# One gather tile in 64 fetched row by row on SyncE's queue, layer 0's last steps reordered, a drain behind the last gather

## The chip, the cores and the metric

The kernel runs on one core of a Trainium2 chip. The metric is device time in microseconds, the median of several executions. A core has five engines that run side by side, each with an instruction queue in order: PE (TensorE, matrix products), DVE (VectorE), ACT (ScalarE), POOL (GpSimd) and SP (SyncE, which only issues transfers). Transfers run on the core's DMA engines and report by semaphores.

## The reference: what is computed

The kernel computes two layers of a relational graph convolution over a graph of 12,500 nodes with 128 features each, 200,000 edges sorted by destination, and 8 edge types (relations), and then a layer norm:

```python
def conv(h, src, dst, et, basis, comp, root, bias):
    W = einsum('rb,bio->rio', comp, basis)            # 8 matrices 128x128
    msgs = einsum('ni,rio->nro', h, W)[src, et]       # one row of 128 per edge
    mean = per (dst, et): sum of msgs / max(count, 1)
    return mean.sum over the 8 relations + h @ root + bias

h = x
for l in range(2):
    h = relu(conv(h, ...layer l...)) + h
out = layernorm(x + h)                                # over the 128 features, eps 1e-5
```

All data is float32. x, src, dst and the edge types are inputs; the weights are basis, comp, root and bias of each layer.

## The kernel before

**Tiles.** The edges are taken in order, 128 to a tile: T = 1563 tiles, the last with 64 edges. Four tiles make a quad (Q = 4, NQ = 391 quads, the last with three tiles), eight make a group (G = 8). The 12,500 nodes make NT = 98 blocks of 128; on average a block's edges fill 16 tiles, that is four quads. Because the edges are sorted by destination, a tile's edges go to few nodes, and the kernel counts on that (a slower `general_path` stands behind a flag that is read at the very end and is not taken here).

**How the work is ordered.** Nearly every operation is recorded in a plan, with what it reads and writes; the plan is then emitted, each engine's operations in the order in which they were recorded, with semaphore waits put in where one operation needs another's result or its buffer. So the order of the Python calls is the order of each engine's queue. Transfers go out on SP's queue through the helper `load` (line 565), which all of them share.

**The gathers.** `gather(l, q)` fetches the rows of one quad, one indirect DMA per tile (line 583): POOL makes the 128 descriptors from 128 indices in SBUF, which lie one per partition. Layer 0 reads rows of x by the edge's source node; layer 1 reads rows of y_d, a DRAM array of 8 x 12,500 rows that layer 0 has written, by source x 8 + type. Behind each gather stands a memset into a scratch tile, `pace` (line 589), 256 columns wide in layer 0 and 200 in layer 1, and each memset waits for the one eight back. The rows of a quad land in one of 14 buffers; gathers are recorded 12 quads ahead of their readers (AHEAD = 12).

**Layer 0** (loop from line 1117). For quad q: `onehot` (DVE, line 873) builds a 128 x 128 matrix per tile from precomputed positions and weights 1/count; `means` (PE, line 914) multiplies the rows by it, ACT copies the result to SBUF; per group `product` (PE, line 938, 16 passes for 8 relations) applies the relation matrices and `place` (PE, line 961) adds the group's result into the block's accumulator. `close_block` (lines 974 to 989) finishes a node block: DVE adds the bias, applies relu and adds the old rows; then three steps are put on the list `todo`, and one is taken from it in each of three quads out of four: `turn` (PE transpose, ACT copy to y_col, store to hT_d), `half(0)` and `half(1)` (PE, line 986: the block times four of layer 1's relation matrices each, into the same PSUM bank pt; ACT copies each to y_row; after the second, one store of the block's 1024 rows to y_d).

**Between the layers.** The loop covers all 391 quads. Behind it stand the place and close of block 96, the last product, the rest of `todo`, and the place and close of block 97. Layer 1's first gather waits for all stores to y_d.

**Layer 1** (loop from line 1163). `onehot` builds 128 x 256 matrices; `add_rows` (PE, line 1028) multiplies a tile's rows by them straight into the accumulator of one block and its neighbour, and adds the block times the root matrix (line 1031) once. `finish(k)` (ACT line 1040, DVE 1047 and 1048) adds what the previous block left over, relu and the old rows; `norm(k)` (PE transpose line 1062, DVE 1063 to 1069, ACT 1066) adds x, applies the layer norm and stores to out. `norm(k)` is recorded behind the first quad of the next block. `load2(k + 1)` fetches the next block's hT_d and x on SP's queue.

**The end.** After the plan the engines meet; a drain of POOL that the framework puts there stands first (line 1185), then each engine reads the flag into a register (line 1212) and branches.

Of the kernel before, what the change touches and what calls it, by code (L numbers as in the profile page):

```python
# [8 lines left out]
F32 = mybir.dt.float32  # L9
# [3 lines left out]
ALU = mybir.AluOpType  # L13
# [286 lines left out]
class Plan:  # L300
# [83 lines left out]
    last = None  # L384
# [31 lines left out]
def ordered_path(  # L416
# [21 lines left out]

    nc = tc.nc
    P = 128
    N, D = x.shape
# [16 lines left out]
    C = P + 2 * HALO  # L460
    S4 = 4
    AHEAD = 12
    H = R // 2
    assert D == P and R * K == P and B == BF + 1 and 1 < TL and LAST < P and BF % 4 == 0
    main = slice(HALO, HALO + P)

    const = ctx.enter_context(tc.tile_pool(name="const", bufs=1))
# [36 lines left out]
    sel = keep([P, G, K], F32, "sel")  # L504
    spread = keep([P, B, GB], F32, "spread")

    PACE, PACED = 8, (2 * P, 200)
    pace = keep([P, PACE, 2 * P], F32, "pace")
    paced = tc.alloc_semaphore("s_paced")
    key = keep([P, 4, C], F16, "key")  # L510
    low = keep([P, 4, C], I32, "low")
    eqs = Ring(const, 2, [P, S4, 4, C], F16, "eq")
    turns = Ring(const, 3, [P, 4, P], F32, "tu")
    rows_r = Ring(const, AHEAD + 2, [P, Q, D], F32, "rows")
    dm_r = Ring(const, 4, [P, Q, 2 * P], F32, "dm")
    sT_r = Ring(const, 3, [P, R, G, K], F32, "sT")
    pl_r = Ring(const, 3, [P, 2 * P], F32, "pl")
# [49 lines left out]
    def copy(out_t, in_t, reads, writes):  # L567
        act(lambda: nc.scalar.activation(out_t, in_t, AF.Copy), reads, writes)  # L568

    rows_g = {}  # L570

    def gather(l, q):
        if q >= NQ:
            return
        t, cell = rows_r.take()
        rows_g[l, q] = (t, cell)
        ids = idx if l == 0 else idy

        def emit():
            ins = []  # L580
            for i in range(q * Q, min((q + 1) * Q, T)):
                m = LAST if i == T - 1 else P
                ins.append(nc.gpsimd.indirect_dma_start(  # L583
                    out=t[:m, i - q * Q, :], out_offset=None, in_=x if l == 0 else y_d,
                    in_offset=bass.IndirectOffsetOnAxis(ap=ids[:m, i:i + 1], axis=0)))
                k = l * T + i
                if k >= PACE:
                    nc.gpsimd.wait_ge(paced, k - PACE + 1)
                nc.gpsimd.memset(pace[:, k % PACE, :PACED[l]], 0).then_inc(paced, 1)  # L589
            return ins  # L590

        b = q * Q // P
        reads = ["idx0" if l == 0 and q == 0 else ("idx", b)] if l == 0 else [("idy", b)]
        if l == 1 and q == 0:
            reads += [("y_d", j) for j in range(NT)]
        plan.add("POOL", emit, reads, [cell], lane="gq", n=min(Q, T - q * Q))

    def weight(l, r):
        c0 = (l * R + r) * NB
# [306 lines left out]
    def means(q):  # L906
        t, c = rows_g.pop((0, q))
        d, dc = dms.pop((0, q))
        s, sc = s_b[q % 2]

        def emit():
            for i in range(in_quad(q)):
                m = LAST if q * Q + i == T - 1 else P
                last = nc.tensor.matmul(s[:, i, :], t[:m, i, :], d[:m, i, :P], start=True, stop=True)  # L914
# [54 lines left out]
    def close_block(j):  # L969
        n = rows_of(j)  # L970
        p, pc = po[j]
        t, c = h_in.pop(j)
        h, hc = h_r.take()
        vec(lambda: nc.vector.tensor_add(h[:n], p[:n], bias_sb[:n]), [pc, "bias"], [hc])  # L974
        vec(lambda: nc.vector.scalar_tensor_tensor(h[:n], h[:n], 0.0, t[:n], op0=ALU.max, op1=ALU.add), [c], [hc])
        pt, pc2 = pt_b
        yc, ycc = yc_r.take()
        yr, yrc = yr_r.take()

        def turn():  # L980
            pe(lambda: nc.tensor.transpose(pt[:, 0, :n], h[:n, :], ident[:n, :n]), [hc, "ident"], [pc2])
            copy(yc[:, :n], pt[:, 0, :n], [pc2], [ycc])
            load(hT_d[j * P:(j + 1) * P, :n], yc[:, :n], [ycc], [("hT_d", j)])

        def half(k):
            pe(lambda: nc.tensor.matmul(pt[:n].rearrange("p r d -> p (r d)"), yc[:, :n],  # L986
                                        w_sb[:, 1, k * H:(k + 1) * H, :].rearrange("p r d -> p (r d)"),
                                        start=True, stop=True),
               [ycc] + [("w", 1, r) for r in range(k * H, (k + 1) * H)], [pc2])
            copy(yr[:n, k * H:(k + 1) * H, :], pt[:n], [pc2], [yrc + (k,)])  # L990
            if k == 1:
                load(y_d[j * P * R:(j * P + n) * R, :].rearrange("(p r) d -> p (r d)", r=R),
                     yr[:n].rearrange("p r d -> p (r d)"), [yrc + (0,), yrc + (1,)], [("y_d", j)])

        todo.extend([turn, lambda: half(0), lambda: half(1)])
# [7 lines left out]
             (ct_b[0].rearrange("p t d -> p (t d)")[:, :2 * P], ct_b[1])]  # L1003

    def load2(k):
        if not 0 <= k < NT:
            return
        n = rows_of(k)
        t, c = hTs[k] = hin_r.take()
        load(t[:, :n], hT_d[k * P:(k + 1) * P, :n], [("hT_d", k)], [c])  # L1010
        t, c = xs[k] = xs_r.take()
        load(t[:n], x[k * P:k * P + n, :], [], [c])

    def add_rows(q, k, opens, last):
# [2 lines left out]
        a, ac = acc[k]  # L1017
        n = in_quad(q)
        root_in = opens and k >= 0
        reads = [c, dc]  # L1020
        if root_in:
            ht, hc = hTs[k]
            reads += [hc, ("w", 1, R)]
# [1 line left out]
        def emit():  # L1025
            for i in range(n):
                m = LAST if q * Q + i == T - 1 else P
                ins = nc.tensor.matmul(a, t[:m, i, :], d[:m, i, :], start=(opens and i == 0),  # L1028
                                       stop=(last and i == n - 1))
# [84 lines left out]
    later = [lambda b=b: check_edges(b) for b in range(B)]  # L1114
    later += [check_span, check_place, check_all]
    later.reverse()
    for q in range(NQ):
        g = q * Q // G
        gather(0, q + AHEAD)
        onehot(0, q + 2)  # L1120
        if q == 1:
            where()
# [22 lines left out]
                parts = None  # L1145
        elif later:
            later.pop()()
    g = NG - 1
# [93 lines left out]
```

## Time and profile before

| | us |
|---|---|
| median of 15 runs | 4561.1 (4553.16 to 4581.48) |
| the profiled execution | 4560.43 |
| its span, first to last instruction | 4558.6 |
| POOL's gathers of layer 0, first to last | 3.45 to 2278.95 |
| POOL's gathers of layer 1, first to last | 2299.56 to 4516.86 |
| last store to out issued | 4540.81 |

| engine | busy us | share of the span |
|---|---|---|
| PE | 2535.3 | 56% |
| DVE | 1708.0 | 37% |
| ACT | 521.3 | 11% |
| POOL | 3939.3 | 86% |

In the profile's lines L583 is line 583 of the kernel; a tile's name stands without its buffer number. "POOL rows L583 <- issue" means that POOL was idle ahead of a gather without waiting for anything that the profile shows; "remote" is a releaser that it could not name. A "q" behind an engine's name (SPq, POOLq) is that engine's sequencer, which issues transfers and runs register and semaphore instructions. All queues together moved 295.88 MB, of which the gathers' software queue had 205.00 MB and kept the 16 DMA engines busy for 15.9% of the span, the other loads and stores 86.62 MB and 5.7%.

### The profile page before, as it was taken

To read this page: it belongs to the slowest core of one execution; us is meant where nothing else is said; L and a number is where in the kernel's file an instruction comes from. 1 tells how busy PE (TensorE), PEld (TensorE's weight loads), DVE (VectorE), ACT (ScalarE), POOL (GpSimd) and SP (SyncE) were. 2 spreads that over 40 slices of the span, in tenths; PEclk is the share of its full clock that TensorE was granted. 3 is DMA by queue.
4 is the path that set the end of the run, shared out by engine and by line. 5 is a ranking of instruction groups with operands and counts; after the bars stand their busy time and mean duration, and the time that the engine had idled before them with its cause. 6 is when DMAs were issued, how large, how long until landed. Compare 5 with 4: busy or idle time off the path is not lost.

```text
span 4558.6 us, 38109 instructions
## 1 busy us (share of the span) xinstructions
PE 2535.3 (56%) x11691; PEld 2045.3 (45%) x11691; DVE 1708.0 (37%) x4724; ACT 521.3 (11%) x1190; POOL 3939.3 (86%) x6260
## 2 busy tenths in 40 slices
PE   4776666666766666666653435435435444435444
PEld 3565555555655555555532324324333333324333
DVE  8772222222222222222232434435334443434434
ACT  0122212222121221211100000000000000000000
POOL 8888888888888888888878888888888888888885
PEclk7998778777788888888776777667667777767767
DMA  3222222222222222222221112111111211112111
GB/s 89 61 84 75 75 74 75 75 75 75 75 80 74 71 75 75 75 75 75 74 60 53 57 53 57 55 53 57 55 54 55 57 55 55 55 54 57 55 53 41
DMA packets 193416, 295.88 MB, mean 65 GB/s; under 512 B 60725, under 2 KB 130687, under 8 KB 193203
## 3 DMA queue, kind: packets, MB, share of 16 engines
q0 software_dynamic: 100032, 205.00, 15.9%
q1 hardware_dynamic: 90650, 86.62, 5.7%
q8 instruction: 96, 1.57, 0.1%
q10 hardware_dynamic: 2521, 1.73, 0.1%
q14 instruction: 117, 0.96, 0.1%
HBM read 229.11 MB, written 64.00 MB: 64 GB/s over the span
## 4 chain that ended last, share of the span: by engine, by line
POOL 40%; another core or an unknown queue 21%; issue 16%; DVE 15%; PE 7%; ACT 1%; DMA 0%; POOLq 0%; ACTq 0%; DVEq 0%; SPq 0%
POOL rows L583 30%; POOL pace L589 10%; DVE dm L873 10%; PE s L1028 2%; PE ct L1028 1%; DVE w_sb L607 1%; PE ct L715 1%; PE ct L716 1%; DVE eq L709 1%; PE s L914 1%; DVE y_col L1047 1%; PE y L938 1%; DVE h L1063 1%; DVE ys L1069 1%
## 5 line engine op out<-in xcount | busy, mean ns | idle before, releaser
L583 POOL DMA_INDIRECT rows<-y_d,idy x1563 | 1489.8, 953 | 309.5 <-issue 254.9
L583 POOL DMA_INDIRECT rows<-in_x_dram,idx x1563 | 1499.6, 959 | 265.0 <-issue 254.3
L589 POOL MEMSET pace<- 128x256 f32 (+1 forms) x3126 | 954.6, 305 | 2.3
L1028 PE MATMUL s<-dm,rows 128*128 128x256 f32 x2086 | 677.3, 487 | 298.5 <-DVE dm L873 171.2
L873 DVE TENSOR_SCALAR dm<-cols,near,w 128x256 f32<-128x256 f32 x1563 | 728.2, 534 | 244.2 <-remote 214.4
L873 DVE TENSOR_SCALAR dm<-cols,kr,w 128x128 f32<-128x128 f32 x1563 | 527.8, 401 | 469.5 <-remote 178.5
L1028 PEld LDWEIGHTS s<-dm,rows 128*128 128x128 f32 x2086 | 510.7, 255 | 423.8 <-DVE dm L873 189.1
L914 PE MATMUL s<-dm,rows 128*128 128x128 f32 x3126 | 536.2, 327 | 290.0 <-DMA rows<-in_x_dram,idx 273.6
L914 PEld LDWEIGHTS s<-dm,rows 128*128 128x128 f32 x3126 | 496.6, 236 | 439.4 <-DMA rows<-in_x_dram,idx 284.6
L938 PE MATMUL y<-w_sb,sT 128*128 128x128 f32 x3136 | 517.5, 335 | 4.4 <-issue 4.2
L938 PEld LDWEIGHTS y<-w_sb,sT 128*128 128x128 f32 x3136 | 507.4, 253 | 6.8 <-issue 6.6
L1062 PE MATMUL po<-ident,y_col 128*128 128x128 f32 x98 | 40.4, 412 | 736.3 <-DVE y_col L1047 368.0
L1028 PE MATMUL ct<-dm,rows 128*128 128x256 f32 x1040 | 329.9, 473 | 181.1 <-DVE dm L873 146.2
L974 DVE TENSOR_TENSOR h<-po,bias_sb 128x128 f32<-128x128 f32 x98 | 28.5, 291 | 949.7 <-PE s L914 431.5
L1062 PEld LDWEIGHTS po<-ident,y_col 128*128 128x128 f32 x98 | 16.2, 165 | 772.4 <-DVE y_col L1047 385.4
L1028 PEld LDWEIGHTS ct<-dm,rows 128*128 128x128 f32 x1040 | 244.9, 247 | 243.2 <-DVE dm L873 157.8
L568 ACT ACTIVATE sT<-s 128x512 f32<-128x512 f32 x391 | 233.4, 597 | 871.6 <-PE s L914 378.3
L961 PE MATMUL po<-ys,pl 128*128 128x128 f32 x780 | 156.6, 331 | 312.7 <-ACT ys L568 271.8
L961 PEld LDWEIGHTS po<-ys,pl 128*128 128x128 f32 x780 | 120.3, 221 | 339.6 <-ACT ys L568 292.5
L986 PE MATMUL pt<-w_sb,y_col 128*128 128x512 f32 x392 | 234.2, 683 | 7.0 <-ACT y_col L568 2.0
L1063 DVE TENSOR_TENSOR h<-po,xs 128x128 f32<-128x128 f32 x98 | 28.2, 288 | 422.3 <-remote 331.3
L1047 DVE TENSOR_TENSOR y_col<-s,hT 128x128 f32<-128x128 f32 x66 | 18.9, 287 | 392.0 <-issue 221.7
(121 smaller groups left out, 1301.1 us busy)
## 6 DMA issues: line engine op xcount, KB each, us to landing
y_d<-y_row SPq DMA_DIRECT2D x97, 512.0 KB
rows<-in_x_dram,idx POOLq DMA_INDIRECT x1563
rows<-y_d,idy POOLq DMA_INDIRECT x1563
h_in<-in_x_dram SPq DMA_DIRECT2D x98, 64.0 KB
h_in<-hT_d SPq DMA_DIRECT2D x98, 64.0 KB
xs<-in_x_dram SPq DMA_DIRECT2D x98, 64.0 KB
hT_d<-y_col SPq DMA_DIRECT2D x97, 64.0 KB
out_dram<-ys SPq DMA_DIRECT2D x97, 64.0 KB
```

Of the source, the lines that this page charges most:

```text
L568: act(lambda: nc.scalar.activation(out_t, in_t, AF.Copy), reads, writes)
L583: ins.append(nc.gpsimd.indirect_dma_start(out=t[:m, i - q * Q, :], out_offset=None, in_=x if l == 0 else y_d, in_offset=bass.IndirectOffse ...
L589: nc.gpsimd.memset(pace[:, k % PACE, :PACED[l]], 0).then_inc(paced, 1)
L873: last = nc.vector.tensor_scalar(t[:, i - q * Q, :wide], cols[:, :wide], ids[:, i:i + 1], w[:, i:i + 1], op0=ALU.is_equal, op1=ALU.mult)
L914: last = nc.tensor.matmul(s[:, i, :], t[:m, i, :], d[:m, i, :P], start=True, stop=True)
L938: last = nc.tensor.matmul(y[:m], t[:, r, :nt, :].rearrange("p t k -> p (t k)"), w_sb[:, 0, r, :], start=(r == 0), stop=(r == R - 1))
L961: last = nc.tensor.matmul(po[j][0][:n], t[:m, k * P:k * P + n], o[:m], start=False, stop=(j in closed))
L986: pe(lambda: nc.tensor.matmul(pt[:n].rearrange("p r d -> p (r d)"), yc[:, :n], w_sb[:, 1, k * H:(k + 1) * H, :].rearrange("p r d -> p (r d)"),
L1028: ins = nc.tensor.matmul(a, t[:m, i, :], d[:m, i, :], start=(opens and i == 0), stop=(last and i == n - 1))
L1047: vec(lambda: nc.vector.tensor_add(v[:, :n], a[:, :n], t[:, :n]), [ac, c], [vc])
L1062: pe(lambda: nc.tensor.transpose(p[:n, :], v[:, :n], ident), [vc, "ident"], [pc])
L1063: vec(lambda: nc.vector.tensor_add(h[:n], p[:n, :], xt[:n]), [pc, xc], [hc])
```

## The change

**One tile in 64 goes another way.** With FAR = 16 quads, the last tile of every sixteenth quad (tile numbers 63, 127, ... up to 1535: 24 of them in each layer) is left out of `gather`, with its memset. Its 128 rows are fetched one by one on SP's queue instead, by `fetch`: at each quad of the loop SP loads BITE = 8 indices from src_i in SBUF into 8 registers, and for each of them computes a row's address and issues a transfer of one row of 512 bytes from x or y_d to one partition of a tile of its own (two such buffers, farSP). Sixteen fetches make a tile; the fetch at quad q belongs to a tile that is read LEAD = 8 quads later, or up to fifteen quads after that for its first pieces. The first eight fetches of each layer are recorded ahead of its loop. `means` and `add_rows` read such a tile from its own buffer and wait for its sixteen pieces.

SP's queue has 14,126 instructions instead of 1,072; POOL's has 48 gathers and 48 memsets fewer. Fetches stand in SP's queue between the stores and loads of their quad, in order with them.

**Indices for layer 1.** One new DVE instruction behind layer 0's loop turns src_i into source x 8 + type in place (128 x 1536).

**Layer 0's last steps.** The loop stops before the last quad. Then: the rest of `todo`, block 96's last product, place and close, `todo` down to one step, the last quad's `means`, that last step, the last product, the place and close of block 97. For the last block the second half goes to the PSUM bank ct instead of pt, DVE copies it instead of ACT, and each half has a store of its own.

**Layer 1.** `load2(1)` is recorded up front with `load2(0)`; in the last quad `norm(96)` stands ahead of `add_rows`.

**The drain.** POOL gets a drain instruction right behind the last gather's quad.

```diff
+    FAR, LEAD = 16, 8
+    BITE = P // FAR
-    PACE, PACED = 8, (2 * P, 200)
+    PACE, PACED = 8, (256, 200)
+    n_paced = [0]
+    far_r = {e: Ring(const, 2, [P, D], F32, f"far{e}") for e in ("SP", "ACT")}
-    plan = Plan(tc, {"hw": 8, "aq": 4, "gq": 3})
+    plan = Plan(tc, {"hw": 8, "aq": 4, "gq": 3, "rSP": 4, "rACT": 4})
+    far_at = {"SP": FAR - 1}
+    row_regs = {e: [plan.engines[e].alloc_register(f"row{k}") for k in range(BITE)] for e in far_at}
+    def far(i):
+        for e, at in far_at.items():
+            if i % (FAR * Q) == at * Q + Q - 1 and i < BF * P and (at == FAR - 1 or i >= FAR * Q):
+                return e
+        return None
+
+    def fetch(e, l, q, part=0, parts=1):
+        s = q + LEAD + FAR - 1 - far_at[e]
+        i, c = (s // FAR * FAR + far_at[e]) * Q + Q - 1, s % FAR
+        if far(i) != e:
+            return
+        if c == 0 and part == 0:
+            far_g[l, i] = far_r[e].take()
+        t, cell = far_g[l, i]
+        n = BITE // parts
+        eng = plan.engines[e]
+        regs = row_regs[e]
+
+        def emit():
+            if part == 0:
+                eng.load(regs, src_i[i % P:i % P + 1, i // P, c * BITE:(c + 1) * BITE])
+            ins = []
+            for k in range(part * n, part * n + n):
+                at = eng.snap(regs[k], min_val=0, max_val=(N if l == 0 else N * R) - 1)
+                p = c * BITE + k
+                ins.append(eng.dma_start(t[p:p + 1, :], (x if l == 0 else y_d)[bass.ds(at, 1), :]))
+            return ins
+
+        reads = [("src", i // P)]
+        if l == 1 and i < 2 * FAR * Q:
+            reads += [("y_d", j) for j in range(NT)] + [("y_d", NT - 1, 1)]
+        plan.add(e, emit, reads, [cell + (c, part)], lane="r" + e, n=n)
+
+    def bits(l, i):
+        return [far_g[l, i][1] + (c, part) for c in range(FAR) for part in range(2)] if far(i) else []
+        tiles = [i for i in range(q * Q, min((q + 1) * Q, T)) if not far(i)]
-            for i in range(q * Q, min((q + 1) * Q, T)):
+            for i in tiles:
-                k = l * T + i
+                k = n_paced[0]
+                n_paced[0] += 1
...
+                rows = far_g[0, q * Q + i][0] if far(q * Q + i) else t[:, i, :]
-        pe(emit, [c, dc], [sc])
+        pe(emit, [c, dc] + bits(0, q * Q + Q - 1), [sc])
...
+            hb, hc2 = ct_b if j == NT - 1 and k == 1 else pt_b
+            if j == NT - 1:
+                if k == 0:
+                    copy(yr[:n, :H, :], hb[:n], [hc2], [yrc + (k,)])
+                else:
+                    vec(lambda: nc.vector.tensor_copy(yr[:n, H:, :], hb[:n]), [hc2], [yrc + (k,)])
+                load(y_d[j * P * R:(j * P + n) * R, :].rearrange("(p r) d -> p r d", r=R)[:, k * H:(k + 1) * H, :],
+                     yr[:n, k * H:(k + 1) * H, :], [yrc + (k,)], [("y_d", j) if k == 0 else ("y_d", j, 1)])
+                return
...
+    for s in range(LEAD):
+        fetch("SP", 0, s - LEAD)
-    for q in range(NQ):
+    for q in range(NQ - 1):
         gather(0, q + AHEAD)
+        fetch("SP", 0, q)
...
+    srcs = [("src", b) for b in range(BF)]
+    vec(lambda: nc.vector.scalar_tensor_tensor(src_i[:, :BF], src_i[:, :BF], float(R), ex[:, :BF, main], op0=ALU.mult,
+                                               op1=ALU.add), ...)
     g = NG - 1
+    while todo:
+        todo.pop(0)()
+    place_in(g - 1)
+    for j in fresh(g - 1):
+        open_block(j)
+    product(g - 1)
     for j in place(g - 1):
         close_block(j)
+    place_in(g)
+    while len(todo) > 1:
+        todo.pop(0)()
+    means(NQ - 1)
+    todo.pop(0)()
     product(g)
-    place_in(g)
-    while todo:
-        todo.pop(0)()
     for j in place(g):
         close_block(j)
...
     load2(0)
+    load2(1)
+    for s in range(LEAD):
+        fetch("SP", 1, s - LEAD)
...
         gather(1, q + AHEAD)
+        if q + AHEAD == NQ - 1:
+            pool(lambda: nc.gpsimd.drain())
+        fetch("SP", 1, q)
...
-        add_rows(q, k, opens, last)
+        if q < NQ - 1:
+            add_rows(q, k, opens, last)
         for d in due:
             norm(d)
         due = []
+        if q == NQ - 1:
+            add_rows(q, k, opens, last)
```

More of the change, by code (lines that the diff above doesn't have):

```diff
@@ L462, in ordered_path @@
     AHEAD = 12
+    FAR, LEAD = 16, 8
+    BITE = P // FAR
     H = R // 2
-    assert D == P and R * K == P and B == BF + 1 and 1 < TL and LAST < P and BF % 4 == 0
+    assert D == P and R * K == P and B == BF + 1 and 1 < TL and LAST < P and BF % 4 == 0 and NQ % 2 == 1
     main = slice(HALO, HALO + P)
@@ L568, in copy @@
         act(lambda: nc.scalar.activation(out_t, in_t, AF.Copy), reads, writes)
-    rows_g = {}
+    rows_g, far_g = {}, {}
+    def far(i):
[29 more added lines that the diff above has]
+        return [far_g[l, i][1] + (c, part) for c in range(FAR) for part in range(2)] if far(i) else []
     def gather(l, q):
@@ L594, in gather @@
         if l == 1 and q == 0:
-            reads += [("y_d", j) for j in range(NT)]
-        plan.add("POOL", emit, reads, [cell], lane="gq", n=min(Q, T - q * Q))
+            reads += [("y_d", j) for j in range(NT)] + [("y_d", NT - 1, 1)]
+        plan.add("POOL", emit, reads, [cell], lane="gq", n=len(tiles))
     def weight(l, r):
@@ L913, in emit @@
                 m = LAST if q * Q + i == T - 1 else P
-                last = nc.tensor.matmul(s[:, i, :], t[:m, i, :], d[:m, i, :P], start=True, stop=True)
+                rows = far_g[0, q * Q + i][0] if far(q * Q + i) else t[:, i, :]
+                last = nc.tensor.matmul(s[:, i, :], rows[:m], d[:m, i, :P], start=True, stop=True)
             return last
-        pe(emit, [c, dc], [sc])
+        pe(emit, [c, dc] + bits(0, q * Q + Q - 1), [sc])
         g = q * Q // G
@@ L985, in half @@
         def half(k):
-            pe(lambda: nc.tensor.matmul(pt[:n].rearrange("p r d -> p (r d)"), yc[:, :n],
+            hb, hc2 = ct_b if j == NT - 1 and k == 1 else pt_b
+            pe(lambda: nc.tensor.matmul(hb[:n].rearrange("p r d -> p (r d)"), yc[:, :n],
                                         w_sb[:, 1, k * H:(k + 1) * H, :].rearrange("p r d -> p (r d)"),
                                         start=True, stop=True),
-               [ycc] + [("w", 1, r) for r in range(k * H, (k + 1) * H)], [pc2])
-            copy(yr[:n, k * H:(k + 1) * H, :], pt[:n], [pc2], [yrc + (k,)])
+               [ycc] + [("w", 1, r) for r in range(k * H, (k + 1) * H)], [hc2])
+            if j == NT - 1:
[6 more added lines that the diff above has]
+                return
+            copy(yr[:n, k * H:(k + 1) * H, :], hb[:n], [hc2], [yrc + (k,)])
             if k == 1:
@@ L1005, in load2 @@
     def load2(k):
-        if not 0 <= k < NT:
+        if not 0 <= k < NT or k in hTs:
             return
@@ L1019, in add_rows @@
         root_in = opens and k >= 0
-        reads = [c, dc]
+        reads = [c, dc] + bits(1, q * Q + Q - 1)
         if root_in:
@@ L1027, in emit @@
                 m = LAST if q * Q + i == T - 1 else P
-                ins = nc.tensor.matmul(a, t[:m, i, :], d[:m, i, :], start=(opens and i == 0),
+                rows = far_g[1, q * Q + i][0] if far(q * Q + i) else t[:, i, :]
+                ins = nc.tensor.matmul(a, rows[:m], d[:m, i, :], start=(opens and i == 0),
                                        stop=(last and i == n - 1))
@@ L1147, in ordered_path @@
             later.pop()()
+    srcs = [("src", b) for b in range(BF)]
+    vec(lambda: nc.vector.scalar_tensor_tensor(src_i[:, :BF], src_i[:, :BF], float(R), ex[:, :BF, main], op0=ALU.mult,
+                                               op1=ALU.add),
+        ends("ex", 0, BF) + [("ex", 0, n) for n in (1, 2, 3)] + srcs, srcs)
     g = NG - 1
+    while todo:
[4 more added lines that the diff above has]
+    product(g - 1)
     for j in place(g - 1):
         close_block(j)
+    place_in(g)
[3 more added lines that the diff above has]
+    todo.pop(0)()
     product(g)
-    place_in(g)
-    while todo:
-        todo.pop(0)()
     for j in place(g):
```

## The prediction

> **What bounds the kernel now.** I read the page's busy times and slices first, then POOL's groups with shapes kept apart and POOL's waits, then a table of windows, the queue's own waits of SP, the chain and timeline at the two ends, and SP's single rows.
>
> The page of before:
> ```profile
> span 4558.6 us, 38109 instructions
> PE 2535.3 (56%) x11691; PEld 2045.3 (45%) x11691; DVE 1708.0 (37%) x4724; ACT 521.3 (11%) x1190; POOL 3939.3 (86%) x6260
> POOL 8888888888888888888878888888888888888885
> ```
> POOL is busy eight tenths of every slice except at the middle and the end. Its groups by form (busy, mean ns, idle before and what ended it):
> ```profile
> L583 POOL DMA_INDIRECT rows<-in_x_dram,idx x1563 | 1499.6, 959 | 265.0 <-issue 254.3 <-PE s L914 8.4 <-DMA idx<-in_src_dram 1.5
> L583 POOL DMA_INDIRECT rows<-y_d,idy x1563 | 1489.8, 953 | 309.5 <-issue 254.9 <-remote 34.0 <-DMA y_d<-y_row 20.6
> L589 POOL MEMSET pace<- 128x256 f32 x1563 | 513.9, 329 | 1.2
> L589 POOL MEMSET pace<- 128x200 f32 x1563 | 440.7, 282 | 1.1
> ```
> The missing tenths are "issue": 254.3 us behind 1563 gathers. So a tile costs POOL (1499.6 + 513.9 + 254.3) / 1563 = 1.451 us in layer 0 and (1489.8 + 440.7 + 254.9) / 1563 = 1.398 us in layer 1. What POOL really waits for is 34.0 us "remote", 20.6 us between the layers and 8.4 us for PE: one run of gathers sets the time. A node block is 16 tiles: 23.22 and 22.37 us.
>
> The windows of both layers (columns: sum, PE, PEld, DVE, ACT, POOL, clock, DMA share, GB/s):
> ```profile
> 3.00:2279.00 2276.00, 1494.47 (x8214) 1243.04 (x8215) 814.93 (x2465) 449.56 (x981) 2010.79 (x3126) 0.81 0.25 75
> 2300.00:4517.00 2217.00, 1013.96 (x3367) 784.93 (x3367) 866.45 (x2184) 64.24 (x191) 1926.90 (x3126) 0.72 0.19 55
> ```
> No other engine is near full. SP's sequencer mostly waits, at its stores, for ACT and DVE:
> ```profile
> SPq L565 <- DVE ys L1069: 826.5, 38, 43.8
> SPq L565 <- ACT y_col L568: 750.3, 62, 105.7
> SPq L565 <- ACT y_row L568: 326.8, 32, 14.0
> ```
> Between the layers and at the very end (timeline, chain, then the lines of the drain and of the final register load):
> ```profile
> 2299.56 0.96 POOL L583 DMA_INDIRECT rows<-y_d,idy  x1 [20.61 <-DMA y_d<-y_row]
> 2295.85 2.96 DMA y_d<-y_row
> L1185 POOLq DRAIN  x1: 8477/8477/8477, 4543.1 to 4543.1; - x1
> L1212 SPq TENSOR_LOAD <-bad x1: 462/462/462, 4551.7 to 4551.7; - x1
> L1212 SPq FUSED_REGOPS  x1: 191/191/191, 4556.2 to 4556.2; - x1
> ```
> POOL ends its gathers at 4516.86, the last out store is issued at 4540.81, and then POOL alone drains for 8.48 us with everybody waiting.
>
> **The change part by part.** The sum is made against the profiled execution, 4560.43 us (span 4558.6 and 1.83 around it), which is 0.7 us under the median of 4561.1.
>
> *POOL's tiles.* 24 of 1563 tiles in each layer leave POOL with their memsets. If POOL stays the bound: 24 x 1.451 = 34.8 us and 24 x 1.398 = 33.5 us. The pacing stays at eight memsets back, now counted without the removed ones.
>
> *SP's fetches.* Each of the first 384 quads of a layer gives SP one load of 8 registers, 8 address instructions and 8 one-row transfers: 13,056 more instructions over the 768 fetches. Nothing in the trace is a transfer from a register's address; the nearest rows are SP's one-partition loads (shortest ex load 0.253 us), its 128-partition h_in loads (median 0.432), 0.045 between neighbours on the queue, the register instruction at the end (0.191; an assertion beside it takes 0.032) and the one-register load (0.462). With c the price of a fetch:
> - lowest: 8 x (0.253 + 0.045 + 0.032 + 0.045) + 0.462 + 0.045 = 3.51 us
> - taken: 8 x (0.253 + 0.045 + 0.191 + 0.045) + 0.507 = 4.78 us, as a transfer of one row is nearest to the one-partition loads and the register instruction is of the kind that forms the address
> - highest: 8 x (0.432 + 0.045 + 0.191 + 0.045) + 8 x 0.462 + 0.045 = 9.45 us, if every register costs a whole load.
>
> SP's own work per block stays: 0.32 + 0.32 + 0.43 + 3 x 0.045 = 1.21 us (hT_d, y_d, h_in) in layer 0; 0.43 + 0.43 + 0.34 + 0.135 = 1.34 us (h_in, xs, out) in layer 1. The new block periods are 63/64 of the old, 22.85 and 22.02 us, so four fetches fit while c is at most (22.85 - 1.21) / 4 = 5.41 and (22.02 - 1.34) / 4 = 5.17 us. At 4.78, SP is 89% and 93% full: it fits, narrowly. That is the whole question of this change.
>
> The Trainium skill ("Runtime: NRT & Kernel Launch", section "Instruction fetch mechanics") speaks against it: a register load costs about 200 ns per register even in bulk. By that, c would be an estimated 4.27 + 1.6 + 0.045 = 5.92 us, SP would be too slow in both layers, and the time about 4965 us. The row here, 0.462 us for one register, shows a start-up part but not what seven more add.
>
> What stands behind SP's fetches: in layer 0 the hT_d and y_d stores, which nobody reads before layer 1, and h_in loads with three blocks in hand; in layer 1 h_in and xs of the next block and the out stores. A fetch serves a tile eight quads on, 8 x 5.5 = 44 us ahead of its reader; SP's stops (the longest for ys 43.8 us) are for work that PE reaches before those quads, so they make no fetch late. The first eight fetches of a layer (38 us) stand behind all loads of the start in SP's order and their tile is wanted only at quad 15, some 80 us in: nothing. PE's wait for the landed rows is one more wait, on a landing long past: nothing while SP keeps ahead.
>
> *The address op.* One DVE instruction over 128x1536. The nearest row, a 128x512 op of the same kind, takes 0.68 us; three times that is 2.0 us, in a stretch where DVE idles 12.19 us before the last close: nothing, 2 us if that cover goes.
>
> *Layer 0's last steps.* From the landing of the last gather (2280.05) to the landing of the last y_d store (2298.81) the chain is 18.8 us, nearly all PE and ACT in turn. All that PE did it does still; product(194) and block 96's place, turn and first half go ahead of the last quad's means. PE was busy up to 2280.09, so this work does not fall into a hole: it only moves. What goes is two waits of PE for a y_row copy (0.66 us between the halves of block 96, 0.66 between those of block 97, now in two banks with two engines): 1.3 us. Bounds: nothing, and 6.1 us if the moved work were all done by 2280 (1.13 means, 1.02 half, 1.88 product, 0.34 + 0.45 copy and place, 0.76 DVE, 0.60 turn, 2.83 halves, 0.62 copy, 2.96 store = 12.7 us left). Below nothing is possible by some 0.5 us: a second y_d store is 0.32 more on SP.
>
> *The drain.* Placed behind the last gather, it runs from 4516.9 to 4525.4, while PE still works until 4538.8; nothing is queued behind it. The drain at the end then finds POOL empty; the other engine's row there, ACT's, shows 8 ns. Gain 8.4 us; bounds nothing (it costs 8.48 again) and 8.5.
>
> *norm(96) ahead of the last add_rows.* PE's transpose for 96 moves from 4535.88 to about 4535.3, DVE's six steps end near 4537.4 rather than 4537.9, where the last block's y_col starts: 0.5 us. Bounds 0 and 1.
>
> **Sum.** 34.8 + 33.5 + 1.3 + 8.4 + 0.5 = 78.5; 4560.4 - 78.5 = 4482 us.
>
> **The rivals.**
> *B: layer 1 gives its share back.* PE trails the landings there: ACT's hT (L1040) waits 1160.4 us for PE in the records, its blocks start between 8.4 and 47 us apart in the timeline, and POOL's 34.0 us "remote" are the places where its ring of 14 quads was full. Today PE catches up at 8.4 us a block; SP, at 4 x 4.78 + 1.34 = 20.5 us, would hold it to that, 1.5 us of gain a block. Then a late spell lasts longer and POOL stops more. If that eats the 33.5 us: 4515 us (4500 to 4550). Against it: PE is busy 1014 of 2217 us.
>
> *C: SP becomes the bound (the other side).* Place: SP's queue, which carries four fetches a block in order. Above 5.4 us every block lasts 4c plus SP's own work. Against before: 96 x (4c + 1.21 - 23.22 + 4c + 1.34 - 22.37) - 10.2 = 0 at c = 5.39 us, 0.61 above my value. Each 0.1 us more costs 77 us: with h_in's 0.432 per transfer c is 6.21 and the time 5187; with 0.462 per register and the rest as taken, c is 8.02 and the time 6577. For it: eight transfers, eight register instructions and a load are each priced from one or two rows. Against: the price taken already holds 0.191 for what may be a plain multiply.
>
> *D: it does not do what it says.* POOL's pace could come from what the gathers meet on the way: if each of the remaining ones slowed by 22 ns (1.4 us / 64) because of 6144 further transfers, the row gains would be gone and 10 us would be left: about 4550. Against it: the DMA share is 0.19 to 0.25, and the rows are the same ones.
>
> **How the numbers follow.** A (SP keeps up) 0.47, with a range of its own of 4465 to 4500: PE's lag at the end is some 17 us of the tail now and may fall anywhere between 2 and 30, and the drain and the seam may each give nothing. B 0.21, C 0.27, D 0.05. The forecast is A's 4482. Below 4465 I leave 0.04; upward B and D take it to 4550 and the cheap part of C (c up to 5.5: 4561 + 0.11 x 770 = about 4645) to 4640, so that some 0.17 of C lies above. A measurement of this kernel tells about 0.2%, 9 us, from no change. Faster: A, B and about half of D, 0.70; same: the rest of D and a sliver of C, 0.04; slower: 0.26.
>
> **What would show it.** Right: POOL has 48 gathers and 48 memsets fewer at the same 959 and 953 ns; SP's fetch, from one register load to the next, takes under 5.1 us and SP still waits for ACT and DVE; the layers last about 2241 and 2184 us; the POOL drain at the end is short and another stands at the last gather. B: POOL's "remote" stops grow past 34 us. C: SP's queue waits for nobody, PE's means wait for the far tile's transfers, blocks last over 23 us. Wrong I would be first through the register load and the transfer from a register's address.

## The result and the profile after

The changed kernel takes 4857.1 us (median of 9 runs, 4838.8 to 4878.2) against 4561.7 us before: 1.0653 times as long, 95% interval 1.0638 to 1.0667. The forecast was 4482 us; the rival with SP as the bound, held at 0.27, is what came. The profiled execution's span is 4863.3 us, 304.7 more than before.

Where the time came from, by the starts of POOL's gathers in both traces:

| stretch | before | after | change | forecast |
|---|---|---|---|---|
| first to last gather of layer 0 | 2274 | 2311 | +37 | -34.8 |
| last gather of layer 0 to first of layer 1 | 22 | 51 | +29 | -1.3 |
| first to last gather of layer 1 | 2216 | 2447 | +231 | -33.5 |
| last gather to the end | 43 | 51 | +8 | -8.9 |

The page after (span, engines, POOL's tenths, and the chain that ended last by engine):
```profile
span 4863.3 us, 57294 instructions
...
PE 2409.2 (50%) x11691; PEld 1970.6 (41%) x11691; DVE 1706.0 (35%) x4726; ACT 513.6 (11%) x1189; POOL 3876.4 (80%) x6164
...
POOL 8788888888888888888577777777777777777774
...
SPq 33%; PE 24%; issue 23%; another core or an unknown queue 12%; DVE 4%; POOL 2%; ACT 2%; DMA 0%; POOLq 0%; DVEq 0%; ACTq 0%
```
POOL falls to seven tenths in layer 1. The chain, which POOL led with 40% before, now runs through SP's sequencer with 33%. POOL's groups by form, then its waits:
```profile
L630 POOL DMA_INDIRECT rows<-in_x_dram,idx x1539 | 1475.3, 959 | 334.2 <-issue 234.8 <-PE s L963 40.0 <-remote 39.3
L630 POOL DMA_INDIRECT rows<-y_d,idy x1539 | 1466.4, 953 | 600.0 <-PE po L1121 248.2 <-issue 239.4 <-remote 60.5
```
```profile
POOL rows L630 <- PE po L1121: 248.2, 47, 22.8
POOL rows L630 <- remote: 99.8, 91, 1.5
POOL rows L630 <- DMA y_d<-y_row: 49.6, 1, 49.6
POOL rows L630 <- PE s L963: 40.0, 34, 6.7
```
The gathers are 24 fewer a layer and as long as before (959 and 953 ns). In layer 1 POOL now stops because its ring of buffers is full. PE, which empties it, waits for the block's h_in, and SP, which loads h_in, hardly waits for anyone (waits of PE, then the queue's own of SP):
```profile
PE s L1087 <- DMA h_in<-hT_d: 794.3, 50, 21.1
PE ct L1087 <- DMA h_in<-hT_d: 488.5, 26, 89.9
```
```profile
SPq L572 <- ACT y_col L575: 74.3, 10, 39.6
SPq L572 <- ACT y_row L575: 47.0, 18, 7.4
SPq L572 <- DVE ys L1128: 19.2, 4, 8.1
```
Before, those three waits of SP were 750, 327 and 827 us: its idle time is gone. From one register load to the next, SP takes 4.2 us when nothing disturbs it, but 5.9 us on average in layer 0 and 6.3 in layer 1 (32 quads in some 188 and 201 us; these hold a quarter of a block's own loads and stores each). The fetch alone, from its load's start to the end of its eighth transfer, takes 5.44 and 5.99 us on average over the 384 of each layer. What differs shows in two windows of neighbouring blocks (timeline of SP, then a table of the two windows, columns as in the prediction's table of windows, then lines of ACT's and POOL's timeline):
```profile
3500.19 4.44 SPq L606 DMA_DIRECT2D farSP<-y_d  x9
...
3533.61 7.84 SPq L606 DMA_DIRECT2D farSP<-y_d  x6
```
```profile
3500.47:3504.68 4.21, 0.00 (x0) 0.00 (x0) 1.45 (x4) 0.00 (x0) 3.71 (x7) 0.50 0.16 48
3532.90:3541.50 8.60, 8.07 (x31) 6.14 (x29) 4.89 (x13) 0.29 (x1) 7.61 (x13) 0.85 0.17 47
```
```profile
3548.66 0.28 POOL L637 MEMSET pace<- 128x200 f32 x1
3550.14 0.37 ACT L1099 ACTIVATE hT<-s,bias_t 128x128 f32<-128x128 f32 x1 [13.43 <-remote]
3550.37 0.95 POOL L630 DMA_INDIRECT rows<-y_d,idy  x1 [1.43 <-remote]
```
POOL gathers in both windows. In the first PE stands still, and nine transfers are issued in 4.44 us. In the second PE works off its backlog, and six take 7.84 us: single register moves and address instructions, 29 and 44 ns otherwise, then take or wait about 0.7 us each. ACT's step behind PE is late too: PE's last product before it ended at 3541.1, and ACT starts at 3550.14, in a stop of POOL of 1.43 us. That is the rule in this trace: of layer 1's 47 starts of this step that are put down to "remote", 43 fall into a stop of POOL longer than 0.6 us.

The two windows differ in PE, so it could be PE's work alone that slows SP. The fetches of layer 1 in the same trace speak against it. Where POOL was busy for less than half of a fetch (48 fetches), it took 4.35 us on average, although PE was busy for 78% of that time. Where POOL was busy for 80% or more, it took 4.78 us with PE at under 5% (141 fetches) and 9.08 us with PE at 80% or more (55 fetches). So in this trace the slowing goes with POOL's work, and it is larger where PE works too; E10's trace has the same order (4.54, 5.53 and 6.46 us).

The drains (the new one behind the last gather, and the one of the framework):
```profile
L1247 POOLq DRAIN  x1: 12217/12217/12217, 4809.7 to 4809.7; - x1
L1268 POOLq DRAIN  x1: 41/41/41, 4855.3 to 4855.3; - x1
```
8.48 us at the end have become 0.04: this step did what was forecast, and PE's longer backlog hides it in the total. The new drain's record of 12.2 us begins before the last gathers run; it ends 8.3 us behind the last gather's end (4813.6).

### The profile page after: what moved, and what is told of

Read it like the earlier page. It is cut to its first block, busy times and chain, and to the rows that moved or that the text cites. A ratio compares the mean times of both kernels' runs of the same rounds, so it can differ in the third digit from the quotient of the medians.

```text
span 4863.3 us, 57294 instructions
## 1 busy us (share of the span) xinstructions
PE 2409.2 (50%) x11691; PEld 1970.6 (41%) x11691; DVE 1706.0 (35%) x4726; ACT 513.6 (11%) x1189; POOL 3876.4 (80%) x6164
## 4 chain that ended last, share of the span: by engine, by line
SPq 33%; PE 24%; issue 23%; another core or an unknown queue 12%; DVE 4%; POOL 2%; ACT 2%; DMA 0%; POOLq 0%; DVEq 0%; ACTq 0%
SPq L606 20%; PE s L963 7%; PE y L987 7%; SPq L604 6%; SPq L601 5%; PE pt L1036 4%; PE po L1010 3%; SPq L572 2%; POOL rows L630 2%; ACT sT L575 1%; DVE dm L921 1%; PE po L947 1%; DVE w_sb L655 1%; PE ct L763 1%
## 5 line engine op out<-in xcount | busy, mean ns | idle before, releaser
L630 POOL DMA_INDIRECT rows<-in_x_dram,idx x1539 | 1475.3, 959 | 334.2 <-issue 234.8
L1087 PE MATMUL s<-dm,rows 128*128 128x256 f32 x2054 | 625.0, 457 | 957.0 <-DMA h_in<-hT_d 794.3
L1087 PEld LDWEIGHTS s<-dm,rows 128*128 128x128 f32 x2054 | 454.3, 234 | 1074.0 <-issue 984.8
L963 PEld LDWEIGHTS s<-dm,rows 128*128 128x128 f32 x3078 | 486.8, 232 | 116.0 <-issue 105.7
L963 PE MATMUL s<-dm,rows 128*128 128x128 f32 x3078 | 497.3, 315 | 1.1 <-DVE dm L921 0.8
L1010 PE MATMUL po<-ys,pl 128*128 128x128 f32 x780 | 182.2, 372 | 636.3 <-ACT ys L575 443.4
L987 PE MATMUL y<-w_sb,sT 128*128 128x128 f32 x3136 | 462.1, 310 | 15.9 <-issue 10.8
L987 PEld LDWEIGHTS y<-w_sb,sT 128*128 128x128 f32 x3136 | 447.2, 227 | 23.9 <-issue 16.9
L1125 ACT ACTIVATE st<-st,eps 128x1 f32<-128x1 f32 x98 | 28.9, 295 | 1545.4 <-DVE st L1124 1057.5
L575 ACT ACTIVATE y_row<-pt 128x512 f32<-128x512 f32 x195 | 116.3, 596 | 187.9 <-PE pt L1036 69.8
L575 ACT ACTIVATE ys<-y 128x128 f32<-128x128 f32 x196 | 54.3, 277 | 764.3 <-remote 540.6
```

Of the source, the lines that this page charges most:

```text
L630: ins.append(nc.gpsimd.indirect_dma_start(out=t[:m, i - q * Q, :], out_offset=None, in_=x if l == 0 else y_d, in_offset=bass.IndirectOffse ...
L963: last = nc.tensor.matmul(s[:, i, :], rows[:m], d[:m, i, :P], start=True, stop=True)
L987: last = nc.tensor.matmul(y[:m], t[:, r, :nt, :].rearrange("p t k -> p (t k)"), w_sb[:, 0, r, :], start=(r == 0), stop=(r == R - 1))
L1010: last = nc.tensor.matmul(po[j][0][:n], t[:m, k * P:k * P + n], o[:m], start=False, stop=(j in closed))
L1087: ins = nc.tensor.matmul(a, rows[:m], d[:m, i, :], start=(opens and i == 0), stop=(last and i == n - 1))
```

## The experiments

The runs stood on several chips, and the kernel before sorts them into two kinds: on the chips of E1 to E4 and of E11 to E14 it took 4498 us (4496 to 4503 over all its runs there), on all others 4642 to 4644. The 4562 of the prediction's pair lies between. Every ratio below is against the kernel before on the same chip. Each chip was used in one session only, so that it is the chip, and not something else in the surroundings of a session, is not shown; "chip of the first kind" and "second kind" stand for what the kernel before took there.

### Without the rows: E1, E11, E17

```diff
-    far_at = {"SP": FAR - 1}
+    far_at = {}
```
with the calls of `fetch` left out.

> No tile is fetched row by row: POOL gathers all 1563, and only the new order of layer 0's last steps, the loads of block 1 up front, norm(96)'s place, the index op on DVE and the drain remain. Theory (SP's queue is full, and that is the whole loss): 4561 - 10 = 4551 us, between 4545 and 4556, with POOL's drain at the end below 0.1 us and the seam between the layers near 20 us again. Rival (the new order or the early drain costs part of the 295 us): above 4570, with a seam that stays near 50 us.

> No rows on SP, the rest of the change as it is. Where the kernel before takes 4560 us or more, theory (the new steps' order and the early drain bring their 10 us anywhere, and all of the loss is SP's row work): 0.993 to 0.999 times the kernel before. Rival (the new order lengthens the seam there, where PE is late): 1.000 to 1.010.

> No rows on SP, the rest of the change as it is. Where the kernel before takes 4560 us or more, theory (all of the loss is SP's row work; the rest brings its 10 us anywhere): 0.993 to 0.999 times the kernel before. Rival (the new order lengthens the seam there, where PE is late): 1.000 to 1.010. Where the kernel before takes 4498 us: 0.998 again.

Measured: 4486.8 against 4498.0 (0.9976, 0.9966 to 0.9985); 4488.2 against 4498.4 (0.9977, 0.9968 to 0.9987); 4633.7 against 4642.0 (0.9979, 0.9968 to 0.9990). The new order and the drain bring 8 to 11 us on chips of both kinds, where 10.2 were forecast, and the whole loss is in the rows. E11 fell on a chip of the first kind, where its two theories do not part; E17 parts them. Waits of E11 (first kind) and of E17 (second kind) differ in this:
```profile
ACT hT L1099 <- PE s L1087: 998.8, 65, 21.4
ACT hT L1099 <- PE ct L1087: 508.1, 33, 20.4
```
```profile
ACT hT L1099 <- remote: 1277.1, 69, 41.8
POOL rows L630 <- remote: 75.6, 49, 2.8
POOL rows L630 <- DMA y_d<-y_row: 55.0, 1, 55.0
```
On the first kind ACT starts when PE's product ends, and the records name PE. On the second ACT starts later than any recorded end, so the wait is "remote", POOL's ring fills now and then, and the seam lasts 55 us rather than 19, without a single row on SP. The trace of before, with its 1160.4 us of "remote", is of this sort, but its seam lasted 22 us; what the kernel before has there on a chip of the second kind no trace shows.

### Half the rows: E2, E7

```diff
-    FAR, LEAD = 16, 8
+    FAR, LEAD = 32, 8
```

> One tile in 128 row by row, 4 rows to a fetch: SP's load is halved. Theory (SP's queue is full): a fetch of 4 rows takes about 0.8 + 4 x 0.42 = 2.5 us undisturbed and some 3.5 us beside the gathers, four of them and SP's own 1.34 us make 15 us of a block of 22.2, so POOL is the bound again: 4561 - 12 x (1.451 + 1.398) - 10 = 4517 us, between 4505 and 4535; PE's wait for h_in nearly gone. Rival (rows fetched beside the gathers slow POOL or PE however few): half of the loss stays, about 4700.

> One tile in 128 row by row, 4 rows a fetch. On a chip where the kernel before takes some 4500 us: 0.990 times it, as before. On one where it takes 4560 or more and a fetch of 8 rows took 5.9 us. Theory (there SP's own instructions are slowed and 4 fetches of 5.9 us fill its queue): 4 rows take about 3.3 us, a block some 14.5 us of SP's time, POOL is the bound: 0.99 times the kernel before (0.980 to 0.997). Rival (rows beside the gathers cost PE and POOL time there, however few): about 1.03.

E2, first kind: 4452.6 against 4498.0 (0.9899, 0.9883 to 0.9916); 45.4 us faster, where the sum of 24 tiles and the other steps was 44. E7, second kind: 4661.8 against 4642.2 (1.0040, 1.0027 to 1.0054): a miss of the theory, which had SP with room to spare at half the rows. SP's waits in E7:
```profile
SPq L572 <- ACT y_col L575: 291.0, 57, 63.6
SPq L572 <- ACT y_row L575: 240.9, 52, 9.7
SPq L572 <- DVE ys L1128: 23.9, 4, 8.9
```
In layer 1 SP is nearly out of idle time (23.9 us for ys) even at 13 instructions a fetch instead of 25: half the rows cost 0.6% against none (1.0040 against 0.9979), where POOL's share would have been a gain of 0.75%. A fetch of 13 instructions took 5.30 us on average there, where 3.3 were expected and E2 took 2.29: half the instructions cost nearly as much time as 25 did in the changed kernel.

### The loads of layer 1 two blocks ahead: E3, E6

```diff
-            load2(k + 1)
+            load2(k + 2)
```

> In layer 1 the loads of h_in and xs are recorded two blocks ahead of their reader instead of one; SP's work is the same. Theory (SP's queue is full: 4 fetches of some 5.9 us and 1.34 us make the block of 25.1 us): no change, 4840 to 4870; PE's wait moves from h_in to the far tile's rows or to the buffers. Rival (the queue has room, but h_in stands behind four fetches and comes late, so that PE and SP wait for each other in turn): layer 1 goes back to about 22 to 23 us a block, 4590 to 4680.

> Layer 1's loads two blocks ahead, once more. Theory (h_in's place in the queue is the loss): 0.983 times the kernel before, in whatever surroundings; where that takes 4562, about 4485. Rival (SP's queue is full where its instructions are slowed down): 0.983 where the kernel before takes 4498, but above 1.03 where it takes 4562.

E3, first kind: 4421.8 against 4498.0 (0.9831, 0.9815 to 0.9848), 76.2 us faster, where this kernel's sum is 78.5. Taken alone it looked like a proof of the rival, that h_in stood too late in the queue. E6, second kind: 4925.0 against 4644.1 (1.0582, 1.0534 to 1.0631), next to 1.0650 for the changed kernel on the same chip; PE still waits 696.8 + 385.2 us for h_in. So the earlier place brings 20 us at most there, and the rival falls: a load two blocks early is late too when the queue is full. What E3 showed alone was the chip, not the edit.

SP's address instructions and transfers (min/median/max in ns), first of the changed kernel in the prediction's pair, then of E3 on a chip of the first kind:
```profile
L604 SPq FUSED_REGOPS  x6144: 1/44/1043, 19.8 to 4822.7; - x199
L606 SPq MOVE farSP<-y_d x3072: 1/29/1394, 2365.7 to 4822.7; - x192
L606 SPq DMA_DIRECT2D farSP<-y_d x3072: 1/227/1391, 2365.8 to 4822.8; - x192
```
```profile
L604 SPq FUSED_REGOPS  x6144: 44/44/60, 19.7 to 4324.2; - x199
L606 SPq MOVE farSP<-y_d x3072: 29/29/29, 2253.1 to 4324.3; - x192
L606 SPq DMA_DIRECT2D farSP<-y_d x3072: 224/228/299, 2253.2 to 4324.4; - x192
```
The same instructions, the same medians; in E3 nothing ever stretches them. It is the chip that differs: in E6, the same program as E3 on the second kind, the address instructions reach 1193 ns and the moves 1379.

### Rows at fixed addresses: E4, E8

```diff
-                eng.load(regs, src_i[...])
-                at = eng.snap(regs[k], ...)
+                at = (i * 8 + p * 97) % N if l == 0 else (i * 64 + p * 777) % (N * R)
-                ins.append(eng.dma_start(t[p:p + 1, :], (x if l == 0 else y_d)[bass.ds(at, 1), :]))
+                ins.append(eng.dma_start(t[p:p + 1, :], (x if l == 0 else y_d)[at:at + 1, :]))
```

> The same 6144 one-row transfers, from rows fixed when the kernel is built, so without register load, moves and address instructions (the rows of the far tiles are then wrong ones). Theory (SP's queue is full through the number of its instructions): a fetch takes 8 x 0.28 = 2.2 us undisturbed, a block 10 to 14 us of SP's time, POOL is the bound: 4482 us, between 4470 and 4500. Rival (the transfers themselves or their traffic are what is slow): 4750 to 4860.

> The same 6144 one-row transfers from rows fixed at build (the far tiles' rows are wrong ones), 8 instructions a fetch instead of 25. Where the kernel before takes some 4500 us: 0.983 times it, as before. Where it takes 4560 or more. Theory (each of SP's instructions is slowed by about the same): a fetch costs about 8/25 of 5.9 = 1.9 to 3 us, SP has room: 0.983 times the kernel before (0.975 to 0.995). Rival (the transfers are what is slow): 1.05 and more, with fetches above 5 us.

E4, first kind: 4420.4 against 4498.0 (0.9830, 0.9813 to 0.9846). E8, second kind: 4626.4 against 4642.2 (0.9961, 0.9949 to 0.9973), and SP waits 299.3 us for ys again. With all 6144 transfers kept, but 8 instructions a fetch instead of 25, the loss of 6.2% (E10, the same chip) is gone. So the rows' traffic is not what costs; it is the other 17 instructions of a fetch: the register load, the address instructions and the moves. The register load alone is not it: in layer 1 it took 0.68 us on average in the changed kernel and 0.80 in E3. Nor is there a fixed price for each instruction: the eight transfers of a fetch took 3.65 us in layer 1 in E8 and 2.35 in E4, and 13 instructions took 5.30 in E7. The rival's "1.05 and more" falls, and so does the theory's 0.983: POOL's 48 tiles fewer should bring 1.5 points over the kernel without rows (0.9979), and bring 0.2.

### The changed kernel elsewhere: E5, E10, E15

> The changed kernel as it is, beside its variant with the layer-1 loads two blocks ahead and the kernel before. In the runs so far the kernel before took 4498 us where the others stood, against 4562 where the changed kernel was first measured, with the same pace of POOL. Theory (the loss is h_in's place behind four fetches in SP's queue, in whatever surroundings): about 1.06 times the kernel before, 4750 to 4860. Rival (the loss comes only where SP's instructions are slowed down, as in the first surroundings, with 5.9 us for a fetch instead of 4.2): 0.983 times the kernel before, where that takes 4498.

> The changed kernel as it is. Where the kernel before takes 4560 us or more: 1.065 times it, with fetches of 5.9 us in layer 1 and SP hardly waiting. Where it takes some 4500 us. Theory (SP's queue is full only where its instructions are slowed): 0.983 times the kernel before, with fetches of 4.2 to 5 us. Rival (h_in's place behind four fetches costs in any case): above 1.00 there.

> The changed kernel as it is. Where the kernel before takes 4560 us or more: 1.062 to 1.066 times it. Where it takes 4498 us. Theory (SP's queue is full only where its instructions are slowed): 0.983 times it, 4421 us, fetches of 4.2 to 5 us, as with the loads two blocks ahead. Rival (there h_in's place behind four fetches is the cost, and the loads two blocks ahead took it away): above 4498.

Measured, all three on chips of the second kind: 4945.4 against 4644.1 (1.0650, 1.0624 to 1.0675), 4932.0 against 4642.2 (1.0624, 1.0596 to 1.0653), 4949.2 against 4642.3 (1.0656, 1.0633 to 1.0678). The ratio of the first pair repeats on three chips. None of these runs fell on a chip of the first kind; the nearest that did are E12 and E14 below.

### A wider gap behind each gather: E9, E14, E16, E12, E18, E13

```diff
-    PACE, PACED = 8, (256, 200)
+    PACE, PACED = 8, (384, 384)
-    pace = keep([P, PACE, 2 * P], F32, "pace")
+    pace = keep([P, PACE, 3 * P], F32, "pace")
```
(280, 224) in E14 and E16, (304, 248) in E12 and E18, and (304, 248) in the kernel before in E13.

> The changed kernel with a pacing memset of 384 columns behind each gather in both layers (256 and 200 before), so that POOL takes about 0.11 us longer a tile in layer 0 and 0.155 in layer 1: 403 us more if POOL were the bound all along. Theory (SP's instructions are slowed by POOL's gathers, so a wider gap helps SP): a fetch falls from 5.9 to 5 us or less where it was 5.9, POOL's waits for PE go away, and the time is 4482 + 403 = 4885 us less what the gap frees. Rival (SP is as slow whatever POOL does): a fetch still takes 5.9 us, and the block of layer 1 stays at 25 us.

> The changed kernel with memsets of 280 and 224 columns (20 ns a tile, 62 us if POOL is the bound). Theory: 4420 + 62 = 4482 us if 20 ns are enough to let SP's instructions through, with fetches under 5 us; otherwise between 4482 and 4932, in the order of the spacing: slower than 304 and 248 where that one is not yet free of stops.

> The changed kernel with memsets of 280 and 224 columns. Where the kernel before takes 4498 us: 4482 again. Where it takes 4560 or more. Theory (the spacing decides): fetches fall from 5.9 toward 5 us and the time lies between 4482 and 4932, below the changed kernel on the same chip; 4482 if 20 ns are enough. Rival: no faster than the changed kernel there, as 20 ns of gap are not what counts.

> The changed kernel with a pacing memset of 304 columns in layer 0 and 248 in layer 1 (48 more in each, 40 ns a tile, 3078 tiles: 125 us if POOL is the bound). Theory (POOL's spacing decides whether SP's and PE's signals get through): with the wider gap of 384 a fetch took 4.3 us and POOL waited for nobody; if 40 ns are enough, 4420 + 125 = 4545 us and fetches under 5 us; if not, SP is still the bound and the time lies between 4600 and 4900. Rival (it takes the whole 0.11 to 0.155 us): above 4820.

> The changed kernel with memsets of 304 and 248 columns. Where the kernel before takes 4642 us: with 280 and 224 columns it took 4897, with 384 in both 4819 and free of stops. Theory (the spacing decides, 40 ns may be enough): between 4545, free of stops, and 4860; fetches between 4.3 and 5.7 us. Rival (layer 1 needs a gap of more than 40 ns): above 4860. Where the kernel before takes 4498: 4545 again.

> The kernel before with the same longer memsets. Theory (it too is held up by late signals of PE where it takes 4640 us, by some 145 us against the 4498 of a chip without them): POOL's stops go, and the time is 4498 + 125 = 4623 us there, a little faster than with the shorter memsets. Rival (it is POOL's work alone that takes longer on that chip): 4642 + 125 = 4767 us. Where the kernel before takes 4498: 4623.

E9, second kind: 4819.3 against 4642.2 (1.0375, 1.0349 to 1.0400). POOL does some 400 us more work than in the changed kernel, and the time is 113 us shorter than that kernel's 4932.0 on the same chip. POOL's groups, its largest stops for others, and ACT's wait in E9:
```profile
L630 POOL DMA_INDIRECT rows<-y_d,idy x1539 | 1463.3, 951 | 271.1 <-issue 253.1 <-DMA y_d<-y_row 17.8 <-PE po L1121 0.2
L637 POOL MEMSET pace<- 128x384 f32 x3078 | 1339.0, 435 | 1.9
```
```profile
POOL rows L630 <- DMA y_d<-y_row: 17.8, 1, 17.8
POOL rows L630 <- DMA idx<-in_src_dram: 1.5, 1, 1.5
```
```profile
ACT hT L1099 <- PE s L1087: 939.6, 56, 24.6
```
A fetch is back at 4.3 us (the median from load to load in layer 1; 6.05 for the changed kernel on that chip), the seam at 18 us, "remote" is gone, and ACT again starts when PE ends. Nothing but the memsets' length was changed, so this shows the cause: POOL's gathers, at the spacing that the memsets give them, slow SP's instructions and PE's signals on these chips; 0.11 us more per tile in layer 0 and 0.155 in layer 1 free both. It is not the memsets that slow SP, as they are longer here. Whether it is the gather instruction or the transfers that it starts is not separated: both come less often with a wider gap.

Less does not free them: 20 ns a tile give 4896.5 against 4642.3 (E16: 1.0537, 1.0501 to 1.0574), which is still 53 us less than the changed kernel on that chip (4949.2, E15), so E16's rival, that 20 ns do nothing, falls; 40 ns give 4883.7 against 4642.0 (E18: 1.0527, 1.0487 to 1.0567), with SP waiting 19.7 and 19.8 us for ys as ever, and fetches of 6.00 us on average in layer 1 in both. The hope of 4545 us on this kind of chip failed.

On the first kind the gap is only time added: E14 4481.7 against 4498.4 (0.9963, 0.9949 to 0.9977), E12 4545.0 (1.0105, 1.0088 to 1.0122), E13 4627.1 (1.0285, 1.0268 to 1.0302), each within 5 us of the sum of POOL's work. E14 and E12 are the changed kernel with h_in one block ahead, and lie 61 and 125 us above the 4420 of E4, as 62 and 125 were expected. In E12 PE waits 2.8 us for h_in in all, and a fetch takes 4.25 us in layer 1. So on these chips h_in's place costs nothing, and the changed kernel itself would be expected near 4421 us, 0.983 times the kernel before; that run is missing. E13 fell on the first kind, so whether the kernel before gains from a wider gap on the second is not measured.

No version here is the best on both kinds: without the rows the time is 0.998 on each; E3 is at 0.983 on the first kind and loses 6% on the second.

## Why the prediction was wrong

**What bounds the kernel now: too simple.** POOL's own row was read rightly, 1.451 and 1.398 us a tile: on chips of the first kind every sum from it held within 5 us. But "one run of gathers sets the time" overlooked what those gathers do to others. The sign was on the table: ACT's 1160.4 us "remote", in waits of up to 32.6 us, were read as waits for PE and used for a rival on PE only. The records of before name PE for few of them:
```profile
ACT hT L1040 <- remote: 1160.4, 70, 32.6
ACT hT L1040 <- PE s L1028: 76.6, 9, 23.8
```
So the sign that something holds up signals between engines while POOL gathers was there, and was not taken.

**The price of a fetch: the step that failed.** The sum's 4.78 us, added up from single rows of SP, is even above the undisturbed price: 4.24 us (E3, layer 1), from a load of 8 registers at 0.79 (0.46 taken), an address instruction at 0.044 (0.191 taken), a move at 0.029 (not foreseen; it makes a fetch 25 instructions, where 17 were counted) and a transfer at 0.228 (0.253 taken), 0.42 a row where 0.53 were taken. What was missing is that the price is not constant: beside the gathers, in the changed kernel, a fetch averaged 5.44 us in layer 0 and 5.99 in layer 1. Against the limits of 5.41 and 5.17 us that just fails in layer 0 and clearly fails in layer 1, and "SP keeps up", on which the forecast stood, falls with it. Where SP is not slowed, the forecast's ratio comes: 4482 is 0.983 of 4560, and E3 and E4 measure 0.983 on the first kind.

**Rival C, from this price, comes near the result.** 96 x (4 x 5.44 + 1.21 - 23.22) = -24 and 96 x (4 x 5.99 + 1.34 - 22.37) = 281, in all +257 us for the two layers; measured +268, but as +37 and +231. So layer 1's loss is SP's price. Layer 0's is not accounted for by it: POOL waited there 40.0 us for PE and 39.3 for "remote" (8.4 and none before), and what makes PE late there stays open. C's mechanism, SP as the bound, was named rightly, but two things were not: PE waited for h_in and not for the far tile's transfers, and the instructions, feared as dear ("0.462 per register"), were cheap but slowed down. The highest price, 9.45 us, stood as a bound, and about one fetch in eight passed 10 us in layer 1, at its start up to 20 from load to load; but the value was taken by the nearest row, and the range ended at c = 5.5.

**The register load.** The Trainium skill ("Runtime: NRT & Kernel Launch", section "Instruction fetch mechanics") has about 200 ns a register, by which eight would take an estimated 1.6 us; that page speaks of loads from HBM, and these read SBUF. The trace has a median of 0.79 us for eight and 0.55 for four (E2), so about 60 ns for each further one. The estimate of 5.92 us a fetch that the prediction drew from it came out next to layer 1's measured mean by luck.

**SP's order of work.** "Nothing" was charged for h_in and xs behind the fetches. That was right where the queue has room (E12, E14) and is where the loss appears where it has none; moving them brings 20 us of some 300 (E6).

**The seam and the end.** The order of the last steps, the drain and norm(96) together: forecast 10.2 us, measured 11.2, 10.2 and 8.3 (differences of the medians in E1, E11 and E17). Their parts were not measured apart, but the drain's 8.48 us fell to 0.04. In the changed kernel the seam grew by 29 us and the end by 8. PE came late to both; that the new order has no part in it is not shown, as the seam is 55 us in E17 too, without the rows, but 18 in E9, with the same order and the wider gap.

**POOL's tiles.** 34.8 + 33.5 us forecast: E3 against E1, on one chip, 4421.8 - 4486.8 = 65 us, where E3's POOL waits for nobody. The mechanism and its size were right where SP keeps up.

## What to carry to other kernels

An engine that mostly waits is not free of charge: price an instruction for it by rows from beside the work that it will stand beside, and look for other engines' late starts ("remote" waits behind a recorded end) as a warning that something there is already short. When work moves from one queue to another, compute the share of the receiving queue and ask what happens if each instruction costs a quarter more; at 90% the answer decides the sign. And run a small gain on more than one chip before believing it.

## What the runs showed of the hardware that was not expected

- One pair of kernels, two signs by chip: the kernel before at 4498 us on some and 4642 on others, with gathers of the same 0.95 us on both (E11 and E17); E3's program at 0.983 on one and, as E6, 1.058 on another.
- On the slower chips POOL's gathers, 0.95 us with gaps of 0.49 in layer 0 and 0.44 in layer 1, hold up register moves of 29 ns on SP by about 0.7 us, and the signals that ACT waits for by 9 us in the spell shown (PE's end at 3541.1, ACT's start at 3550.1). When POOL stops, both come through: fetches of 4.35 us, and 43 of 47 late starts of ACT inside such a stop (45 of 47 in E16, but only 16 of 45 in E18). Gaps of 0.60 us end the slowing (E9); 0.53 and 0.48 do not (E18). On which path SP's instructions and PE's signals meet the gathers no record shows, nor why chips differ; this stays open.
- A first drain of POOL behind gathers takes 8.5 us although the last gather ended 27 us before it (the kernel before), and ends 8.3 us behind the last gather where it stands right behind it (the changed kernel, whose record of 12.2 us starts earlier); a second one takes 0.04.
